# Attention with a paged cache: queries and own keys transposed in VectorE blocks and carried by the cached keys' copies, two pairs ahead, with the rope tables kept in DRAM

## The chip, the cores and the metric

The kernel runs on one core of a Trainium2 chip. The core's engines work side by side, each through its own list of instructions in order: TensorE (PE, with its weight loads shown as PEld), VectorE (DVE), ScalarE (ACT), GpSimd (POOL) and SyncE (SP), which here only issues DMA transfers. SBUF is the on-chip memory of 128 partitions, PSUM the memory that TensorE writes. The metric is the device time of one execution in microseconds.

## The reference, cut to what matters

A block on x of shape 8 x 128 x 512, all in float32. A first layer applies a weight matrix chosen for each batch row, then a causal attention with 32 heads of 16, and adds x. A second layer attends with 32 query heads and 8 key heads of 128 over 512 cached positions and the 128 own ones; then comes a feed-forward product with low-rank additions, and x is added again.

```python
q = _rmsnorm(q, q_norm_w)
k = _rmsnorm(k, k_norm_w)
q = _rope(q, pos)
k = _rope(k, pos)
kc = k_cache[block_table].reshape(bsz, L, HK, D)
vc = v_cache[block_table].reshape(bsz, L, HK, D)
k_all = jnp.concatenate([kc, k], axis=1)
v_all = jnp.concatenate([vc, v], axis=1)
scores = jnp.einsum('bqhd,bkhd->bhqk', q, k_all) * SCALE
scores = jnp.where(valid[:, None, None, :], scores, -1e+30)
probs = jax.nn.softmax(scores, axis=-1)
o = jnp.einsum('bhqk,bkhd->bqhd', probs, v_all)
```

The change touches the second attention: how rotated queries and own keys get their depth onto the partitions, as the score product needs it, and where the cosine and sine tables of `_rope` are kept.

## The kernel before, in words

**Stages.** Stage one (lines 276 to 801, up to about 220 us) computes the first layer, batch row by batch row, and prepares the second: rope tables (`angles`, `tables`), page indices, merged low-rank matrices (`merge_loads` and its followers). Stage two (from line 804) is the second attention with the feed-forward part.

**Units.** Stage two is cut into N = 64 units, one for each key head g and batch row b. Two units with neighbouring key heads and the same row are a pair: unit u = 2n + m is half m of pair n, and a gathered page of the cache holds both heads. Heads go in four groups of 16 units: units 0 to 15 have g = 0 or 1, and so on. A unit projects its queries (four heads, `q_matmul`) and own key and value (`kv_matmul`), computes scores against 512 cached and 128 own keys, softmax, values, and the output projection, which is added up over g in `y_acc`. Rows that have had their last head (g = 7, from unit 49 on) pass through `ffn_flip`, `ffn_lora` and `ffn`.

**The loop.** The order on every engine is the order of the code (`manual_schedule`); semaphores are derived from the tiles. Iteration u of the loop at line 1052 runs: `scores(u)`, with the query product of unit u + 1 between the four heads (`between`); `kv_matmul` and `kv_turn` of u + 1; `values(u - 1)`; `norms`, `queries` of u + 1; for odd u `turn_keys` of pair u // 2 + 2; the gathers on POOL; `out_proj(u - 1)`; `own_keys(u + 1)`; weight loads; the feed-forward part.

**Queries and own keys.** `q_turn` multiplies the projection in PSUM by the tables (three DVE operations), POOL adds the halves into `qa`, ACT squares for the norm; `kv_turn` does the same for the key, `ka`, and copies the value to `vo`. `norms` computes the reciprocal roots on POOL. `queries` transposes `qa` by four TensorE transposes against the identity and one ACT copy into `qT`; `own_keys` does one transpose and one copy into `kTo`. The score products of line 889 (cached keys) and 896 (own keys) take `qT` as stationary operand, loaded anew for each of the two passes of a float32 product.

**Cached keys.** `turn_keys(n)` has DVE transpose the gathered keys of pair n in blocks of 32 x 32 into `flk`, of which there is one buffer. `move_keys(n, a)` issues four transfers on SP that carry the blocks to their partitions in `kT2` (two buffers), in runs of 256 bytes. `pair_keys`, called after the third head of `scores`, issues eight of them in each unit, for the next pair. The first two pairs use TensorE instead (`keys`).

**Probabilities.** After the division DVE transposes each head's probabilities in blocks into `flips` (one buffer), and 16 transfers on SP carry them to `pT`, which `values` reads one iteration later.

**SP's queue.** In each iteration: eight kT moves, then 16 pT moves, then loads of weights or feed-forward rows if any are due. It is one queue in order; a transfer that waits holds the later ones.

**Buffers.** `tile_a` is a ring of 12 buffers of 2 KB a partition that serves stage one (gathered conditioning weights `cw`, the merge inputs `la`, `lb`, `las`, `lbs`, `gs`) and stage two (`sq`, `qa`, `qb`, `qT`, `oT` and others). A new tile waits until the oldest one's readers are done. The score and value products share two PSUM buffers (`p_sc`), so that the score product of a third head waits for the softmax pass (line 902) of the first.

## Time and profile before

| | |
|---|---|
| median of three runs | 1414.55 us (1414.14 to 1414.56) |
| profiled execution | 1423.96 us, span 1421.1 us |
| PE busy | 1391.5 us, 98% |
| DVE busy | 931.8 us, 66% |
| ACT busy | 655.9 us, 46% |
| POOL busy | 568.2 us, 40% |
| query transposes, L254 | 256, 38.5 us |
| own-key transposes, L271 | 64, 17.5 us |
| cached keys by DVE blocks, L840 | 120, 42.8 us |
| kT moves on SP, L853 | 480 of 32 KB |
| pT moves on SP, L936 | 1008 of 80 KB |

Busy time is the time in which an engine has an instruction running; instructions of TensorE overlap, so the distance between starts, not the duration, tells what one costs. A timeline line gives the start and length in microseconds, the engine, the line of the kernel, the operation, what it writes from what, its shapes and its count; in brackets stands the idle time before it and what ended it. A line of the windows view gives a stretch, its length, the busy time and count of PE, PEld, DVE, ACT and POOL, the granted TensorE clock (1.00 is full), the DMA share and GB/s.

### The profile page before, as it was taken

To read this page: it belongs to the slowest core of one execution; us is meant where nothing else is said; L and a number is where in the kernel's file an instruction comes from. 1 tells how busy PE (TensorE), PEld (TensorE's weight loads), DVE (VectorE), ACT (ScalarE), POOL (GpSimd) and SP (SyncE) were. 2 spreads that over 40 slices of the span, in tenths; PEclk is the share of its full clock that TensorE was granted. 3 is DMA by queue.
4 is the path that set the end of the run, shared out by engine and by line. 5 is a ranking of instruction groups with operands and counts; after the bars stand their busy time and mean duration, and the time that the engine had idled before them with its cause. 6 is when DMAs were issued, how large, how long until landed. Compare 5 with 4: busy or idle time off the path is not lost.

```text
span 1421.1 us, 20290 instructions
## 1 busy us (share of the span) xinstructions
PE 1391.5 (98%) x6244; PEld 898.5 (63%) x6244; DVE 931.8 (66%) x2266; ACT 655.9 (46%) x1520; POOL 568.2 (40%) x553
## 2 busy tenths in 40 slices
PE   6999989999999999999999999999999999999998
PEld 6877755566666666666666666666666665666555
DVE  5777846566666666666666666666666665666651
ACT  3555535444444444444444444444444444344431
POOL 5774342433333333333333333333333433343220
PEclk9999999999999999999999999999999999999999
DMA  6255013444444565444445654444456544444440
GB/s 198 75 164 183 31 37 104 129 117 118 119 115 119 161 193 151 119 119 119 119 119 159 196 148 119 118 119 119 121 160 192 152 117 136 131 111 112 115 111 30
DMA packets 156202, 180.26 MB, mean 127 GB/s; under 512 B 92416, under 2 KB 97792, under 8 KB 156096
## 3 DMA queue, kind: packets, MB, share of 16 engines
q1 hardware_dynamic: 140544, 134.39, 34.0%
q0 software_dynamic: 15552, 44.58, 10.8%
q8 instruction: 50, 0.82, 0.2%
q14 instruction: 56, 0.46, 0.1%
HBM read 75.83 MB, written 4.72 MB: 57 GB/s over the span
## 4 chain that ended last, share of the span: by engine, by line
PE 93%; DVE 2%; issue 2%; DMA 1%; ACT 1%; POOL 1%; SPq 1%; another core or an unknown queue 0%; DVEq 0%; POOLq 0%; ACTq 0%
PE op L963 19%; PE qp L177 15%; PE sc L889 15%; PE yp L982 15%; PE kvp L217 7%; PE sc L896 4%; PE fp L1044 2%; PE hp L514 2%; PE qTp L254 2%; PE pT1p L638 2%; PE qp L530 2%; PE att L673 2%; PE o L657 1%; PE sc L595 1%; PE kvp L545 1%
## 5 line engine op out<-in xcount | busy, mean ns | idle before, releaser
L902 DVE CUSTOM_DVE_ANT_0 pr<-sc,mask,nq 128x640 f32<-128x640 f32 x256 | 226.0, 884 | 144.2 <-PE sc L896 90.9
L912 ACT ACTIVATE pr<-pr,nm 128x640 f32<-128x640 f32 x256 | 211.8, 827 | 189.3 <-DVE nm L902 102.1
L889 PE MATMUL sc<-kT,qT 128*128 128x512 f32 x512 | 262.0, 593 | 0.0
L177 PE MATMUL qp<-wq,x1T 128*128 128x512 f32 x512 | 251.2, 593 | 0.0
L963 PE MATMUL op<-pT,vg 128*128 128x256 f32 x1024 | 242.0, 379 | 1.6 <-DMA pT<-fl 1.6
L203 POOL TENSOR_TENSOR qa<-qa,qb 128x512 f32<-128x512 f32 x64 | 81.8, 1278 | 375.2 <-DVE sums L879 375.2
L982 PE MATMUL yp<-wo,oT 128*128 128x512 f32 x504 | 229.2, 598 | 2.0 <-DVE oT L971 2.0
L963 PEld LDWEIGHTS op<-pT,vg 128*128 128x128 f32 x1024 | 193.9, 190 | 27.8 <-DVE sums L879 1.8
L880 ACT ACTIVATE pr<-pr,sums 128x640 f32<-128x640 f32 x256 | 208.4, 814 | 0.0
L883 DVE STREAM_TRANSPOSE fl<-pr 128x640 f32<-128x640 f32 x252 | 189.2, 808 | 0.0
L896 PEld LDWEIGHTS sc<-kTo,qT 128*128 128x128 f32 x512 | 96.4, 190 | 124.4 <-issue 119.2
L982 PEld LDWEIGHTS yp<-wo,oT 128*128 128x128 f32 x504 | 91.4, 191 | 95.1 <-issue 91.5
L160 POOL DMA_INDIRECT kg<-in_k_cache_dram,idx_kv x128 | 131.6, 1029 | 35.3 <-issue 34.8
L160 POOL DMA_INDIRECT vg<-in_v_cache_dram,idx_kv x128 | 128.6, 1005 | 37.8 <-issue 33.6
L889 PEld LDWEIGHTS sc<-kT,qT 128*128 128x128 f32 x512 | 87.7, 191 | 80.2 <-issue 77.8
L256 ACT COPY qT<-qTp 128x512 f32<-128x512 f32 x64 | 37.5, 586 | 205.3 <-PE qTp L254 204.7
L217 PEld LDWEIGHTS kvp<-wkv,x1T 128*128 128x128 f32 x512 | 97.3, 190 | 40.5 <-issue 30.1
L217 PE MATMUL kvp<-wkv,x1T 128*128 128x256 f32 x512 | 121.0, 379 | 0.0
L244 POOL TENSOR_TENSOR rs<-ss,minus_half 128x5 f32<-128x5 f32 x64 | 76.5, 1196 | 83.1 <-DVE ss L242 82.2
L177 PEld LDWEIGHTS qp<-wq,x1T 128*128 128x128 f32 x512 | 82.8, 191 | 31.5 <-issue 31.5
L896 PE MATMUL sc<-kTo,qT 128*128 128x128 f32 x512 | 99.2, 275 | 0.0
L273 ACT COPY kTo<-kTp 128x128 f32<-128x128 f32 x64 | 17.1, 267 | 166.4 <-issue 115.2
(155 smaller groups left out, 1701.1 us busy)
## 6 DMA issues: line engine op xcount, KB each, us to landing
pT<-fl SPq DMA_DIRECT2D x1008, 80.0 KB
kT<-flk SPq DMA_DIRECT2D x480, 32.0 KB
wq<-in_wq_dram SPq DMA_DIRECT2D x8, 1024.0 KB
wo<-in_wo_dram SPq DMA_DIRECT2D x8, 1024.0 KB
wkv<-in_wkv_dram SPq DMA_DIRECT2D x8, 512.0 KB
kg<-in_k_cache_dram,idx_kv POOLq DMA_INDIRECT x128
vg<-in_v_cache_dram,idx_kv POOLq DMA_INDIRECT x128
res<-x_kept SPq DMA_DIRECT2D x8, 256.0 KB
```

Source lines behind the costliest of these rows:

```text
L160: nc.gpsimd.indirect_dma_start(out=dst[:, c].rearrange("p n d -> p (n d)"), out_offset=None, in_=src, in_offset=bass.IndirectOffsetOnAxis( ...
L177: nc.tensor.matmul(s["qp"][:].rearrange("p h d -> p (h d)"), x1T[b][:, c, :], weights[g][0][:, c, :], start=(c == 0), stop=(c == KC - 1),)
L203: nc.gpsimd.tensor_tensor(qa[:], qa[:], qb[:], ALU.add)
L217: nc.tensor.matmul(s["kp"][:], x1T[b][:, c, :], weights[g][1][:, c, :], start=(c == 0), stop=(c == KC - 1))
L880: nc.scalar.activation(prs[r][:], prs[r][:], AF.Copy, scale=sums[:, r : r + 1])
L883: nc.vector.transpose(s["flips"][:, :, :, r, :].rearrange("p b c j -> p c b j"), prs[r][:])
L889: nc.tensor.matmul(sc[:, : NBLK * P].rearrange("p (k j) -> p k j", j=32), s["qT"][:, r, :], s["kT"], start=True, stop=True,)
L896: nc.tensor.matmul(sc[:, NBLK * P : NK], s["qT"][:, r, :], s["kTo"][:], start=True, stop=True)
L902: nc.vector.tensor_tensor_reduce(out=pr[:], in0=sc[:, :NK], in1=mask[:], scale=s["nq"][:, r : r + 1], scalar=3.0e38, op0=ALU.add, op1=ALU.min,
L912: nc.scalar.activation(pr[:], pr[:], AF.Exp, bias=nm[:, r : r + 1], scale=-1.0, accum_out=sums[:, r : r + 1],)
L963: nc.tensor.matmul(ops[h][:, : 2 * S], cached(u, "vg", c) if c < NBLK else s["vo"][:], s["pT"][:, :, c, 2 * h : 2 * h + 2, :].rearrange("p ...
L982: nc.tensor.matmul(yp[:], s["oT"][:, r, :], weights[g][2][:, r, :], start=(r == 0), stop=(r == REP - 1))
```

## The change

From pair 2 on (units 4 to 63) queries and own keys go the way of the cached keys. `flk` and `kT2` grow from 4 to 9 rows of blocks (`ROWS`): four for cached keys, four for the query heads, one for the own key. `turn_ahead(v)` adds two DVE block transposes that write unit v's queries, interleaved with those of its pair's other unit (a step of two elements), and its own key into `flk`. The eight transfers for a pair's half stay as many, each with 9 rows in place of 4. The score products read queries and own keys from `kT2`. TensorE transposes remain for units 1 to 3 (and unit 0 in stage one).

So that a pair is ready in time, projection runs four units ahead: iteration u projects u + 4; iteration 0 projects 1, 2 and 3, iteration 1 projects 4 and 5, and iterations 60 to 63 project nothing. Weights of queries and keys are loaded three iterations earlier.

The tables are no longer kept in SBUF: stage one builds them in `tab_all`, stores them to DRAM, and `load_tab` brings each pair's 256 KB back into one of two buffers. The `tile_a` ring shrinks to 9 buffers; `las`, `lbs` and `gs` get buffers of their own, and `vo`, `ka` and `nq` more buffers.

```diff
-        return both.tile(shape, F32, tag="a", name=name, bufs=12)
+        return both.tile(shape, F32, tag="a", name=name, bufs=9)
...
+    tab_kept = dram.tile([B, P, 4, D2], F32, tag="tab", name="tab_kept")
+    tabs = {}
...
+    def load_tab(n):
+        if n < N // 2:
+            tabs[n] = both.tile([P, 4, D2], F32, tag="tab", name=f"tab_{n}")
+            nc.sync.dma_start(out=tabs[n][:], in_=tab_kept[n % B])
...
-        flk = p2.tile([P, 4, NBLK, 2, 32], F32, tag="flk", name=f"flk_{n}", bufs=1)
+        flk = p2.tile([P, 4, ROWS, 64], F32, tag="flk", name=f"flk_{n}", bufs=1)
...
-        kT = p2.tile([P, NBLK, 4, 2, 32], F32, tag="kT2", name=f"kT2_{n}")
+        kT = p2.tile([P, ROWS, 4, 64], F32, tag="kT2", name=f"kT2_{n}")
...
+            s["kT"] = kT[:, :NBLK, :, own].rearrange("p c a i -> p (c a) i")
+            s["qT"] = [
+                kT[:, NBLK + r].rearrange("p a (i m) -> p (a i) m", m=2)[:, :, m] for r in range(REP)
+            ]
+            s["kTo"] = kT[:, NBLK + REP, :, own]
+
+    def turn_ahead(v):
+        flk, m = pairs[v // 2]["flk"], v % 2
+        nc.vector.transpose(
+            flk[:, :, NBLK : NBLK + REP, :].rearrange("p b r (i m) -> p r b i m", m=2)[:, :, :, :, m],
+            st[v]["qa"][:].rearrange("p r d -> p (r d)"),
+        )
+        nc.vector.transpose(
+            flk[:, :, NBLK + REP, 32 * m : 32 * m + 32], st[v]["ka"][:]
+        )
...
     def pair_keys(u):
         if u == 2:
-            turn_keys(u)
+            turn_keys(2)
+            turn_ahead(4)
         if 1 < u < N - 2:
+            if u % 2 == 0:
+                turn_ahead(u + 3)
             for a in range(u % 2 * 2, u % 2 * 2 + 2):
                 move_keys(u // 2 + 1, a)
...
+        ahead = {0: [1, 2, 3], 1: [4, 5]}.get(u, [u + 4] if u + 4 < N else [])
...
+        def project(v):
+            for c in range(KC):
+                q_matmul(v, c)
+            for part in q_turn(v):
+                part()
+            for c in range(KC):
+                kv_matmul(v, c)
+            kv_turn(v)
...
-            norms(u + 1)
-            queries(u + 1)
...
+            norms(ahead[0])
+        if u == 0:
+            queries(1)
+            keys(1)
+        if u == 1:
+            keys(2)
+            keys(3)
+        if u > 2 and u % 2 and u // 2 + 2 < N // 2:
+            turn_keys(u // 2 + 2)
+            turn_ahead(u + 3)
...
         if u == 0:
+            project(2)
             flip_last(x1_last)
...
-            own_keys(u + 1)
...
+            own_keys(1)
+            norms(2)
+            project(3)
+            queries(2)
+            own_keys(2)
+            norms(3)
+            load_tab(2)
+            load_tab(3)
             load_wo(1)
+        elif u == 1:
+            queries(3)
+            own_keys(3)
+            project(5)
+            norms(5)
+        if u % 2:
+            load_tab((u + 7) // 2)
```

## The prediction

> **What bounds the kernel now.** I read the page first, its busy times and the chain that ended last.
>
> ```profile
> span 1421.1 us, 20290 instructions
> ...
> PE 1391.5 (98%) x6244; PEld 898.5 (63%) x6244; DVE 931.8 (66%) x2266; ACT 655.9 (46%) x1520; POOL 568.2 (40%) x553
> ...
> PE 93%; DVE 2%; issue 2%; DMA 1%; ACT 1%; POOL 1%; SPq 1%; another core or an unknown queue 0%; DVEq 0%; POOLq 0%; ACTq 0%
> ```
>
> PE (TensorE) is the bound nearly everywhere: a microsecond taken from PE shortens the kernel, unless a wait takes its place. Next, the timeline of PE from the end of one unit of the second attention into the next.
>
> ```profile
> 719.46 0.60 PE L254 MATMUL qTp<-ident,qa 128*128 128x128 f32 x4
> 719.90 3.60 PE L982 MATMUL yp<-wo,oT 128*128 128x512 f32 x8
> 723.34 0.27 PE L271 MATMUL kTp<-ident,ka 128*128 128x128 f32 x1
> 723.45 1.02 PE L889 MATMUL sc<-kT,qT 128*128 128x512 f32 x2
> ...
> 726.47 1.02 PE L889 MATMUL sc<-kT,qT 128*128 128x512 f32 x2
> ```
>
> Starts follow each other without a gap. Four query transposes take 719.46 to 719.90, the own-key transpose 723.34 to 723.45. A unit repeats every 17.78 us (719.46, 737.25). Then the same stretch on DVE (VectorE).
>
> ```profile
> 722.01 1.42 DVE L840 STREAM_TRANSPOSE flk<-kg 128x256 f32<-128x256 f32 x4
> 723.54 0.69 DVE L989 TENSOR_TENSOR y<-yp,y 128x512 f32<-128x512 f32 x1
> 724.14 0.55 DVE L874 TENSOR_SCALAR mask<-place,lens_f 128x640 f32<-128x640 f32 x1
> 724.83 0.88 DVE L902 CUSTOM_DVE_ANT_0 pr<-sc,mask,nq 128x640 f32<-128x640 f32 x1
> 725.64 0.08 DVE L902 DVE_READ_ACCUMULATOR2_ANT nm<- 128x1 f32 x1
> ```
>
> After an odd unit DVE works without a pause from L840 to the first softmax pass (L902), which frees the scores' PSUM buffer at 725.72. The third score product needs that buffer and starts at 726.47: 0.75 us of slack, the tightest place of the loop. Last, three places where PE does stand still today: PE's timeline in unit 2 and in unit 63, with SP's timeline for the latter, and the granted clock by windows.
>
> ```profile
> 272.43 5.40 PE L982 MATMUL yp<-wo,oT 128*128 128x512 f32 x8 [2.00 <-DVE oT L971]
> ...
> 1386.44 1.97 PE L963 MATMUL op<-pT,vg 128*128 128x256 f32 x8 [1.57 <-DMA pT<-fl]
> ```
>
> ```profile
> 1374.22 10.25 SPq L936 DMA_DIRECT2D pT<-fl  x16
> ```
>
> ```profile
> 270.00:275.00 5.00, 3.00 (x9) 1.26 (x8) 3.21 (x11) 0.59 (x1) 2.33 (x3) 0.85 0.38 90
> 275.00:280.00 5.00, 5.00 (x15) 2.48 (x14) 1.99 (x4) 0.27 (x1) 3.23 (x4) 0.80 0.71 200
> ```
>
> Two things to keep: a 2.00 us stall was followed by a clock of 0.85 and 0.80, and the next output projection took 5.40 us in place of 3.60, so such a stall costs about 1.8 us again; and from SP's first pT issue to the value product are 12.2 us (1374.22 to 1386.44), sixteen issues of 0.63 us and the landing.
>
> **PE work removed.** L254 and L271 go for units 4 to 63 (1 to 3 keep them). 60 x (0.44 + 0.11) = 60 x 0.54 = 32.5 us, all on the path. ACT's two copies (0.59 + 0.27 us a unit) go too, off the path. Taken alone the unit becomes 17.24 us.
>
> **What replaces it on DVE.** Two block transposes a unit, 512 and 128 columns. Four L883 of 640 columns take 3.00 us, four L840 of 256 take 1.42; that gives a pitch of 0.73 and 0.34 us, 0.08 plus 1.02 ns a column, so 0.60 + 0.21 = 0.81 us. They write with a step of 8 bytes, for which there is no row; I bound them by 0.81 and twice that, and take 0.81, since no L840 or L883 row shows its many short runs costing extra. For odd units they run inside an even unit after the third softmax pass, in a 0.97 us idle stretch of DVE ahead of the fourth: hidden, and with that cover gone the fourth pass only moves into the 0.75 us that DVE idles before the next qp. For even units they stand right after L840, ahead of y, mask and the first softmax pass, in the stretch above. There PE comes 0.54 us earlier and DVE 0.81 us later: 0.75 - 0.54 - 0.81 = -0.60, with 0.06 us of hand-over a stall of 0.66 us. It needs L989 on DVE (for head group 0 ACT copies y, and there DVE idles a further 1.00 us, at 296.99) and no FFN behind the unit (its five products give PE 4.3 us, from 1316.73 to 1321.03). So units 17, 19 ... 49: 17 x 0.66 = 11.2 us lost; at twice the price 25 us.
>
> **Transfers and queues.** Each kT move grows from 128 to 288 packets of 256 bytes. The packet records put 128 in 0.31 us on 16 engines, so 288 in 0.70 us, against an issue pitch of 0.64 us; a unit's eight lag about 1 us at most. Engine time a unit: 1280 packets more at 17.5 ns over 16 engines, 1.4 us, in a stretch whose DMA share is 0.49. SP issues 16 x 0.633 + 8 x 0.64 us plus half a table load, 15.6 us of 17.24. The kT moves of an even unit now wait on SP for the odd unit's turn, about 1 us; behind them are that unit's pT moves, which have 2.5 us of SP idle before (715.5 to 718.0). Issue time does not follow packets: wq with 512 packets issues in 0.43 to 0.53 us, pT with 32 in 0.59. I take nothing; the other end is the third rival. The table load (256 KB for two units) is issued two units ahead and waits for nothing late. The weight loads move with their first use.
>
> [...]
>
> **Stationary queries with a step of 8 bytes.** Every load in the trace is contiguous (190 ns, a new one every 0.108 us behind 128-column passes). Ends: the same rate, 0; half rate, 0.108 us exposed at five loads a unit, 60 x 0.54 = +32 us. I take 0, as the moving kT, already cut in runs of 32, runs at the 593 ns of contiguous qp; that row has no step inside a run, so the other end stays a rival.
> [...]
>
> **The front.** Units 2, 3 and 5 are projected additionally in units 0 and 1: PE work that is only moved. In unit 1, norms(5) and the adds before it come on POOL behind rs(4) and eight gathers of 1.26 us. From the end of the value product: oT and rs(4) 1.9, gathers 10.1, qa, ka, rs 2.9, then nq, ka, mask and softmax on DVE 2.1, together 17.0 us until the buffer is free; PE needs it after key transposes 0.87, yp 3.44, queries 0.54, projection 5.16, two scores 2.15 and a qp pass 0.86: 13.0. So a stall of 4 us at unit 2, then about 1.4 at its yp because 2 x 0.81 us join L840 in the middle of the unit, and 2.2 of low clock; today 2.0 + 1.8 there and 1.3 in unit 0. Net +3, ends 0 and 6.
>
> **Stage one.** With 9 instead of 12 rotating buffers lb_1 to lb_3 wait on SP for the last conditioning (155.4 us, where las waits now), and w_eff and the gate rows queue behind them. DVE reads the gates at 161.6 and would wait some 2 to 3 us; PE has work queued. The 2 MB of tables leave at 92 us, in a slice where DMA is half busy. +2, ends 0 and 5.
>
> **The tail.** Units 60 to 63 project nothing, so PE's 5.16 us there no longer cover the pT moves. Without projection the probabilities are turned 10.45 us after a unit's first score (unit 63: 1379.67, divisions to 1388.4, then the last turns), plus 12.2: values may start 22.7 us after, and SP's kT moves make it 23.3 in unit 60. PE arrives in unit 61 after scores 4.6, values 4.3, yp 3.44, scores 4.6, yT 0.43: 17.4. Stall 5.9. Unit 62 has FFN work before it and waits for nothing; in unit 63 again 22.7 against 17.4, 5.3. Less today's 1.57: +9.6; DVE-bound scores +0.8; low clock after two stalls 2 x 1.8: +3.6. Together +14, ends 8 and 18.
>
> **Sum.** -32.5 + 11.2 + 3 + 2 + 14 = -2.3 us. In the profiled execution 1423.96 us (span 1421.1 and 2.9 around it) becomes 1421.7; that execution lies 9.4 over the median, so I apply the difference to the median: 1414.55 - 2.3, or **1412 us**.
>
> **Rivals.**
> 1. The stalls stay small (a softmax buffer freed in time, PE's stalls at front and tail half of mine, no low clock): 32.5 less about 10, 1392 us. For it: DVE is a third idle. Against: the odd boundary is DVE work end to end. 15%.
> 2. The stepped weight loads run at half rate: it decides once a load takes longer than the 0.108 us pass before it. 1412 + 32 = 1444 us, slower. 11%.
> 3. SP becomes the loop: kT issues at the pace of their packets or worse. It decides at 0.85 us an issue ((17.24 - 10.13 - 0.3) / 8); at 1.2 us a unit takes 20.0 and the kernel 1412 + 60 x 2.8 = 1580 us. Against: wq's issue time. 7%.
> 4. DVE writes with the step at half rate: 14 us more at the boundaries, 1426 us. PE's gain is then a DVE wait, and the change does not do what it says. 10%.
> Mine: 57%, 1412, its own range 1404 to 1420.
>
> **How the numbers follow.** Within 0.2% (2.8 us, about what a measurement of this kernel can tell) means 1411.7 to 1417.4. My case splits 26 / 15 / 16 into faster, same, slower; rival 1 adds 15 faster, rivals 2 and 3 18 slower, rival 4 nearly all slower: 0.41, 0.16, 0.43. The range leaves half of rival 1 below, rival 3 and part of 2 above: 1394 to 1446.
>
> **What would show it.** No L254 and L271 beyond units 1 to 3. Between an odd unit and the next, from unit 17, a gap of about 0.7 us before the third score, released by nm of L902; unit pairs of 35.1 us there and 34.5 in head group 0. PE waits on pT of 5 to 6 us in units 61 and 63, with low clock behind. Loads of the stepped queries at 190 ns. A kT issue of about 0.65 us. Wrong I would be if the loads lengthen, if SP shows no idle time, or if the boundary shows no gap.

## The result and the profile after

The changed kernel takes 1422.21 us (median of six runs, 1418.23 to 1424.01), the kernel before in the same comparison 1413.89 us (six runs, 1412.67 to 1414.56): a ratio of 1.0057, 95% interval 1.0043 to 1.0072, 8.3 us slower. Two repetitions on other chips gave 1.0081 (1.0065 to 1.0096) and 1.0054 (1.0038 to 1.0071). The time lies inside the predicted range (1394 to 1446), but the direction that the forecast leaned to, 2 us faster, is wrong.

The runs below fell on several chips, on which the kernel before took 1413.9 to 1422.6 us, so times are compared within one group of runs only, as ratios, and stretches of the loop by their length. A stretch is read from one profiled execution.

The page of the profile after, for the lines shown of before:

```profile
span 1418.9 us, 19695 instructions
...
PE 1370.0 (97%) x5944; PEld 873.0 (62%) x5944; DVE 977.5 (69%) x2386; ACT 598.2 (42%) x1400; POOL 557.9 (39%) x553
...
PE 65%; SPq 11%; DVE 10%; DMA 9%; issue 3%; POOL 1%; ACT 1%; DVEq 0%; POOLq 0%; ACTq 0%
```

300 matmuls are gone, and PE is busy 21.5 us less. But the chain that ended last, 93% PE before, is now 65% PE, and SP's queue (11%) and transfers (9%) have come in where they had 1% each. DVE rose from 2% to 10%. The rest of this section looks for the places.

**The boundary after an odd unit**, PE's timeline of the changed kernel, at the place that answers the one shown of before:

```profile
662.75 1.02 PE L935 MATMUL sc<-kT 128*128 128x512 f32 x2
663.61 0.39 PE L942 MATMUL sc<-kT 128*128 128x128 f32 x2
663.84 1.03 PE L935 MATMUL sc<-kT 128*128 128x512 f32 x2
...
664.93 1.02 PE L183 MATMUL qp<-wq,x1T 128*128 128x512 f32 x2
666.18 1.14 PE L935 MATMUL sc<-kT 128*128 128x512 f32 x2 [0.23 <-DVE nm L952]
```

and DVE's for the same stretch:

```profile
661.84 1.43 DVE L864 STREAM_TRANSPOSE flk<-kg 128x256 f32<-128x256 f32 x4
663.19 0.67 DVE L885 STREAM_TRANSPOSE flk<-qa 128x512 f32<-128x512 f32 x1
663.78 0.27 DVE L889 STREAM_TRANSPOSE flk<-ka 128x128 f32<-128x128 f32 x1
663.98 0.65 DVE L1039 TENSOR_TENSOR y<-yp,y 128x512 f32<-128x512 f32 x1
664.55 0.54 DVE L920 TENSOR_SCALAR mask<-place,lens_f 128x640 f32<-128x640 f32 x1
665.23 0.88 DVE L952 CUSTOM_DVE_ANT_0 pr<-sc,mask,nq 128x640 f32<-128x640 f32 x1
666.04 0.08 DVE L952 DVE_READ_ACCUMULATOR2_ANT nm<- 128x1 f32 x1
```

The two new transposes, L885 and L889, take 0.79 us from start to next start (663.19 to 663.98), the first softmax pass ends at 666.12, and the third score product starts at 666.18, released by it, 1.25 us after the product ahead of it where two passes back to back take 0.86 (662.75 to 663.61). These pairs repeat every 35.08 us (17.79 + 17.29); in head group 0 a pair takes 34.64 (17.35 + 17.29), against 35.72 before (17.93 + 17.79).

**The weight loads**, SP's timeline of the changed kernel. x8 is one unit's kT moves, x16 one unit's pT moves:

```profile
438.55 0.53 SPq L136 DMA_DIRECT2D wq<-in_wq_dram  x1
439.18 0.50 SPq L137 DMA_DIRECT2D wkv<-in_wkv_dram  x1
439.73 7.34 SPq L896 DMA_DIRECT2D kT<-flk  x8
447.18 10.30 SPq L986 DMA_DIRECT2D pT<-fl  x16
457.58 0.53 SPq L128 DMA_DIRECT2D tab<-tab_kept  x1
458.22 0.39 SPq L136 DMA_DIRECT2D wq<-in_wq_dram  x1
458.70 0.46 SPq L137 DMA_DIRECT2D wkv<-in_wkv_dram  x1
459.25 7.12 SPq L896 DMA_DIRECT2D kT<-flk  x8
466.48 10.60 SPq L986 DMA_DIRECT2D pT<-fl  x16
477.12 5.23 SPq L896 DMA_DIRECT2D kT<-flk  x8
```

SP goes from row to row without a gap from 438.55 to 482; what it waits lies inside the rows. Eight kT moves, 5.23 us at 477.12, take 7.34 and 7.12 us behind a weight load, and the unit from 447.18 to 466.48 costs SP 19.30 us, where PE's shortened unit is 17.3. PE's units there last 18.15 and 19.07 us. In this trace such long units stand in pairs at five of the six places where wq and wkv or wo of two heads are loaded (from 449, 539, 733, 1016 and 1105 us; none at the second loads of wo). There the loop of before has units of its ordinary length but for one, of 19.76 us, at the last loads of wo. What SP waited for in the loop (total us, times, longest):

```profile
SPq L986 <- DVE fl L929: 32.7, 37, 1.9
SPq L896 <- DVE flk L889: 16.3, 16, 2.4
...
SPq L896 <- DMA wkv<-in_wkv_dram: 6.3, 6, 1.6
SPq L896 <- DMA wo<-in_wo_dram: 5.9, 6, 2.3
```

In the traces of this kernel and of the one before, the kT move eight issues behind a load waits until the load has landed, though no data ties the two: here wkv, issued at 439.18, lands at 446.47, and the move eight issues behind it starts at 446.49, where SP was done with the one ahead at 445.64. All 18 kT moves that stand so behind a load in this trace start after its landing, 14 of them within 0.03 us. The wait is not new: before, all 18 start within 0.02 us of it. The same view of the kernel before:

```profile
SPq L936 <- DVE fl L883: 80.9, 39, 2.5
...
SPq L853 <- DMA wkv<-in_wkv_dram: 7.6, 6, 1.4
SPq L853 <- DMA wo<-in_wo_dram: 6.9, 6, 2.4
```

Before, SP waited 80.9 us for turned probabilities (`fl`): it had time left. After, it is 32.7 us, and 16.3 us go to a wait that did not exist, for `flk`, the turned queries and keys.

How PE comes to wait in the two units shown, 18.15 and 19.07 us long:

```profile
453.14 1.13 PE L935 MATMUL sc<-kT 128*128 128x512 f32 x2 [0.52 <-DVE nm L952]
478.80 1.96 PE L1013 MATMUL op<-pT,vg 128*128 128x256 f32 x8 [1.56 <-DMA pT<-fl]
```

The second is a value product whose pT moves are late. The first is a third score that waits for DVE, and DVE is late because `flk` has one buffer: the last kT move that reads it, issued at 446.49, lands at 448.93, and DVE's next transpose into it starts at 449.25, 0.80 us late. Over the whole run that line reads, after and, below, before:

```profile
L864 DVE STREAM_TRANSPOSE flk<-kg 128x256 f32<-128x256 f32 x120 | 42.8, 414 | 5.0 <-DMA pT<-fl 3.6
...
L840 DVE STREAM_TRANSPOSE flk<-kg 128x256 f32<-128x256 f32 x120 | 42.8, 413 | 2.0 <-DMA kT<-flk 0.4
```

(The line after names `pT`. In the stretch shown a pT move lands at 449.25, the very time at which DVE starts, and the last kT move out of `flk` at 448.93; the transpose shares no data with that pT move.) The kT moves are late because they land late behind a load: the fifth of the eight, issued at 442.54, lands at 448.22, after 5.7 us, where the median in the loop is 2.2.

**The front and the tail**, PE's timeline of the changed kernel:

```profile
277.04 2.08 PE L935 MATMUL sc<-kT,qT 128*128 128x512 f32 x2 [3.59 <-DVE nm L952]
290.11 3.67 PE L1032 MATMUL yp<-wo,oT 128*128 128x512 f32 x8 [0.54 <-DVE oT L1021]
...
1335.72 3.70 PE L1032 MATMUL yp<-wo,oT 128*128 128x512 f32 x8 [1.77 <-DVE oT L1021]
1347.33 2.67 PE L1013 MATMUL op<-pT,vg 128*128 128x256 f32 x8 [2.74 <-DMA pT<-fl]
...
1372.77 3.70 PE L1032 MATMUL yp<-wo,oT 128*128 128x512 f32 x8 [1.64 <-DVE oT L1021]
1384.29 1.97 PE L1013 MATMUL op<-pT,vg 128*128 128x256 f32 x8 [2.64 <-DMA pT<-fl]
```

with the granted clock (the number behind POOL's count) in two of these places:

```profile
275.00:280.00 5.00, 2.96 (x5) 1.60 (x6) 3.10 (x9) 2.45 (x5) 0.09 (x1) 0.67 0.00 0
...
1345.00:1350.00 5.00, 2.67 (x9) 2.26 (x10) 3.06 (x8) 3.45 (x7) 0.00 (x0) 0.84 0.59 117
```

To compare runs, the span is cut at the first score product of units 0, 4 and 60. "Front" contains three projections of 5.16 us that the change moved there from the tail (15.48 us).

| run | to unit 0 | front, 0 to 4 | loop, 4 to 60 | tail, 60 to end |
|---|---|---|---|---|
| before | 220.62 | 74.95 | 1025.46 | 100.06 |
| before, repeated (`b_again`) | 223.89 | 72.26 | 1027.01 | 100.06 |
| after | 218.15 | 92.73 | 1013.70 | 94.33 |
| after, repeated (`after_again`) | 224.61 | 93.72 | 1016.55 | 95.99 |
| after, repeated (`after_third`) | 225.50 | 94.19 | 1012.47 | 96.02 |

The loop lost 30.2 us of transposes (56 x 0.54) and got only 9 to 15 us shorter.

### The profile page after: what moved, and what is told of

Its sections match the earlier page's. It is cut to its first block, busy times and chain, and to the rows that moved or that the text cites. A ratio compares the mean times of both kernels' runs of the same rounds, so it can differ in the third digit from the quotient of the medians.

```text
span 1418.9 us, 19695 instructions
## 1 busy us (share of the span) xinstructions
PE 1370.0 (97%) x5944; PEld 873.0 (62%) x5944; DVE 977.5 (69%) x2386; ACT 598.2 (42%) x1400; POOL 557.9 (39%) x553
## 4 chain that ended last, share of the span: by engine, by line
PE 65%; SPq 11%; DVE 10%; DMA 9%; issue 3%; POOL 1%; ACT 1%; DVEq 0%; POOLq 0%; ACTq 0%
PE op L1013 13%; PE qp L183 11%; PE sc L935 10%; SPq L986 10%; PE yp L1032 8%; PE kvp L223 5%; DMA wkv<-in_wkv_dram 3%; PE sc L942 2%; DMA pT<-fl 2%; DVE fl L929 2%; DMA kT<-flk 2%; PE fp L1094 2%; PE hp L526 2%; PE pT1p L650 2%; PE qp L542 2%
## 5 line engine op out<-in xcount | busy, mean ns | idle before, releaser
L952 DVE CUSTOM_DVE_ANT_0 pr<-sc,mask,nq 128x640 f32<-128x640 f32 x256 | 223.4, 883 | 81.6 <-PE sc L942 71.2
L935 PE MATMUL sc<-kT 128*128 128x512 f32 x480 | 248.3, 599 | 8.8 <-DVE nm L952 7.5
L942 PEld LDWEIGHTS sc<-kT 128*128 128x128 f32 x480 | 94.2, 196 | 111.8 <-issue 111.8
L935 PEld LDWEIGHTS sc<-kT 128*128 128x128 f32 x480 | 87.3, 196 | 97.5 <-issue 61.4
L166 POOL DMA_INDIRECT kg<-in_k_cache_dram,idx_kv x128 | 123.9, 968 | 35.3 <-issue 34.6
L942 PE MATMUL sc<-kT 128*128 128x128 f32 x480 | 93.8, 277 | 0.0
L641 POOL TENSOR_TENSOR pr<-pr,sums 128x1024 f32<-128x1024 f32 x32 | 60.0, 1897 | 70.5 <-DVE sums L640 58.6
L630 ACT ACTIVATE pr<-sc,nm 128x128 f32<-128x128 f32 x256 | 67.7, 415 | 33.3 <-DVE nm L616 33.3
```

The costliest lines, as they stand in the source:

```text
L166: nc.gpsimd.indirect_dma_start(out=dst[:, c].rearrange("p n d -> p (n d)"), out_offset=None, in_=src, in_offset=bass.IndirectOffsetOnAxis( ...
L935: nc.tensor.matmul(sc[:, : NBLK * P].rearrange("p (k j) -> p k j", j=32), s["qT"][r], s["kT"], start=True, stop=True,)
L942: nc.tensor.matmul(sc[:, NBLK * P : NK].rearrange("p (a j) -> p a j", j=32), s["qT"][r], s["kTo"], start=True, stop=True,)
L952: nc.vector.tensor_tensor_reduce(out=pr[:], in0=sc[:, :NK], in1=mask[:], scale=s["nq"][:, r : r + 1], scalar=3.0e38, op0=ALU.add, op1=ALU.min,
```

## The experiments

Four questions, by size: the loads, the boundary, the removed work itself, and the two ends.

**Base.** The kernel before once more, and the changed kernel twice.

> The kernel before once more, to see what an ordinary execution of it looks like: its first profiled execution took 1423.96 us where its other runs took 1413 to 1414.6. Theory A (that profile held about 10 us of waits that ordinary executions don't have): this profile's span is 1410 to 1412 us, and against the first one the missing time shows in named places, unit 2 (2.0 us stall and 1.8 us of low clock) and stage one the first candidates. Theory B (the profiler itself adds the 10 us to this kernel): the span is again about 1421 us while the times are 1414 us.

Measured: 1421.77 us, ratio 0.9994 (0.9985 to 1.0004). The span is 1423.2 us where the other runs took 1420 to 1425, so neither theory holds here: on this chip every run is about as long as the first profiled one. The loop of before is the same in both traces but for units 49 and 50 (19.76 and 17.79 us, here 20.75 and 18.35). The front is not: the stall of 2.00 us and the slow output projection at 272.43, which the prediction showed as a standing cost, are absent here (a stall of 1.01 us, the projection at 3.70 us). They belonged to the profiled execution.

> The changed kernel unchanged, beside the kernel before on the same chip, as the base of this group. From the two traces the parts add up to -32.5 us (transposes), +8.5 (boundary), +10 (around the weight loads), +11.3 (tail), +2 to +5 (front), +3 (stage one): +2 to +5 us. The first comparison gave +8.3. If the parts are all of it, the difference here is +2 to +6 us; if a part is missing, it is +8 again.

Measured: 1432.74 against 1420.46 us, ratio 1.0081 (1.0065 to 1.0096): 11.5 us by the ratio. So the parts read from the first pair of traces were too small.

> The changed kernel unchanged, as the base beside the kernel before on this chip: +6 to +12 us, as in the two comparisons so far (ratios 1.0057 and 1.0081), with 8 to 13 us of excess around the weight loads in the loop from unit 4 to 60 (1011 to 1017 us).

Measured: 1429.38 against 1421.27 us, ratio 1.0054 (1.0038 to 1.0071), loop 1012.47 us.

**Do the weight loads cost 10 us, and how?** First the loads were taken away:

```diff
     def load_qkv(g):
+        if g > 1:
+            weights[g] = weights[g - 2][:2]
+            return
...
     def load_wo(g):
+        if g > 1:
+            weights[g].append(weights[g - 2][2])
+            return
```

> The changed kernel without the later loads of wq, wkv and wo: groups 2 to 7 use the weights of the group two before, so the output is not the reference's. Theories A and B: 10 us faster than the changed kernel, all pairs from unit 4 to 60 at 34.6 or 35.1 us. Theory C: no change, the long units stay. If A holds, the kernel with the loads on ACT's queue comes within 2 us of this one; if B, it does not.

Measured: 1419.68 us, ratio 0.9992 (0.9983 to 1.0001), 12.6 us less than the changed kernel in the same group (1.0081 less 0.9992, of 1420). The loop is 1003.64 us, and every pair from unit 4 to 50 has its length of 34.6 or 35.1 us but for one unit of 18.14. This loop is also, to 0.2 us, before's with two other steps applied: 1025.46 - 30.2 + 17 x 0.50 = 1003.8; that it fits so closely is in part luck, as before's loop holds 2.0 us at unit 49, and the changed kernel's units are 0.03 us longer than those of `no_turn` below (17.29 against 17.26). So the excess of the three runs of the changed kernel over it, 10.1, 12.9 and 8.8 us, is what the loads cost. Compared with `no_w` product by product, 5.4, 8.0 and 5.6 us of it stand ahead of value products (pT late) and 4.6, 4.9 and 3.1 us ahead of score products (in the main DVE late). Theory C falls.

The next two put the loads on another queue: `queue = nc.gpsimd if g > 1 else nc.sync` for the first, `nc.scalar` for the second, on wq, wkv and wo.

> The changed kernel with the later loads of wq, wkv and wo issued by POOL in place of SP. Theory A (at the weight loads SP's queue is what delays the pT moves: eight kT moves took 7.3 us there in place of 5.2): units around the loads go from 18.2 to 19.1 us back to 17.3 and 17.8, the time falls by about 8 us, ratio to the kernel before about 1.000. Theory B (the bytes of the weights delay the pT moves whoever issues them): no change, ratio 1.006.

Measured: 1463.43 us, ratio 1.0283 (1.0268 to 1.0298): units of up to 25.56 us where POOL issues a load. PE waits there for moves that SP issued:

```profile
457.60 3.75 PE L1015 MATMUL op<-pT,vg 128*128 128x256 f32 x8 [5.21 <-DMA kT<-flk]
```

POOL's two issues (0.84 and 0.83 us, from 446.24) are short. But the last two pT moves, which SP issued at 447.32 and 447.96, behind the loads, land at 455.14 and 457.04, after 7.8 and 9.1 us, where the median of pT moves in the trace of the changed kernel is 2.4. That fits theory B, by which the loads delay moves whoever issues them, and is far more than it forecast. How large that part is when SP itself issues the loads, ahead of its moves in one queue, this run does not tell.

> The changed kernel, but the later loads of wq, wkv and wo (groups 2 and up) are issued by ACT instead of SP. Theory A (these loads stand in SP's queue ahead of the kT and pT moves, which start late by their issue): units of 18.2 to 19.1 us beside the loads fall back to the 17.8 / 17.3 us of their neighbours, 8 to 10 us faster than the changed kernel. Theory B (their 1 to 2 MB occupy the DMA engines that the 256-byte packets of the kT moves need too, whoever issues them): the excess stays, within 2 us of the changed kernel. Theory C (the excess has nothing to do with the loads): the same as B, and no gain without the loads either.

Measured: 1491.24 us, ratio 1.0499 (1.0486 to 1.0513). What SP waited for in this kernel's loop:

```profile
SPq L988 <- DMA wo<-in_wo_dram: 40.3, 5, 9.1
...
SPq L988 <- DMA wq<-in_wq_dram: 21.5, 3, 8.8
SPq L898 <- DMA wq<-in_wq_dram: 17.3, 3, 6.0
```

SP's moves, which share no data with the weights, wait up to 9.1 us for loads that ACT issued; in the changed kernel, where SP issues the loads, its longest such wait was 2.3 us. So the wait that stood in SP's queue is still there, and longer; what lengthens it was not shown. Neither A nor B is tested by this run; it adds a cost of its own.

Then the loads stayed on SP, in pieces: two halves of wq and of wo and wkv by itself, one piece behind each group of four kT moves or behind eight pT moves.

```diff
                 move_keys(u // 2 + 1, a)
+                next_piece()
...
+            if a == 1:
+                next_piece()
```

> The changed kernel, but SP issues each later load of wq and wo in two halves and wkv by itself, one piece behind each group of four kT moves or behind eight pT moves, in place of 1.5 MB in one go ahead of the kT moves. Theory A (the kT moves wait behind a burst of 5 us of all DMA engines): long units shrink from 18.2 - 21 us to at most 0.5 us over their neighbours, 8 to 11 us faster than the changed kernel, so 0 to +3 us against before. Theory B (the same bytes cost the same wherever they stand, as the queue has no idle time): long units stay, +8 to +12 us against before.

Measured: 1427.83 us, ratio 1.0059 (1.0045 to 1.0073), loop 1011.79 us. `tail_split`, of the same group and with the loads as in the changed kernel, has a loop of 1011.40 us. The spreading brought nothing, as theory B expected. Theory A falls in the form in which I gave it.

A count fits that. Taken from the traces is the time from a unit's last pT issue on SP to the first value product that reads these probabilities; where PE waited for pT it had fallen to 2.3 to 2.7 us, which the landing then took (two numbers where even and odd units differ):

```
                     ordinary units      smallest, beside a load
before               5.4                 3.1
before, no turns     4.9                 2.2   (no_turn, below)
after, group 0       4.9 and 3.5 - 4.2   2.3, with PE waiting
after, later         5.4 and 3.7 - 4.9   2.5, with PE waiting
after, no loads      as after            3.0   (no_w)
```

Beside a load it is smaller by 2.3 us before and 2.7 in `no_turn`. On SP two loads cost about 3 us: 1.0 to 1.2 us of issue and about 2 us more for the eight kT moves behind them, half of which is the wait for the landing of wkv. Before, 5.4 us had room for that. The shorter unit alone takes 0.5 us, and in every second unit about 1 us more goes to the kT moves that wait for the turn (`flk`), ahead of the pT moves.

What of the change used the rest was asked by taking away the additional packets alone (`in_` and `out` of a move cut to the cached keys' rows, `:NBLK`), and the later table loads alone (`tabs[n] = tabs[3]` for n above 3).

> The changed kernel, but the kT moves carry only the cached keys (128 packets of 256 bytes, as before, in place of 288). The turned queries and own keys stay behind, and the scores read four rows of cached keys in their place with the same steps, so the output is not the reference's; turns on DVE, number of SP issues, tables and weight loads are those of the changed kernel. Theory P (the 160 additional packets a move hold the queue, so that behind a weight load the kT and pT moves land late): the excess around the weight loads (8 to 13 us) goes, the loop from unit 4 to 60 takes 1003 to 1005 us. Theory S (SP's issue time, with its waits for the landing of the weights, has too little slack in a unit of 17.3 us, whatever the packets): the excess stays, 1011 to 1017 us.

Measured: 1418.43 us, ratio 1.0023 (1.0010 to 1.0037), loop 1006.87 us: 3.2 us of excess instead of 8.8 to 12.9. At the first load a unit of 19.00 us stays.

> The changed kernel without the table loads behind the fourth: later pairs use the fourth pair's tables, so the output is not the reference's. SP has 0.26 us more a unit and the queue 1.0 us less of transfers every two units. Theory P: 1 to 2 us of the excess go, loop 1010 to 1014 us. Theory S: the slack grows from 1.7 to 1.9 us a unit, 2 to 4 us go, loop 1008 to 1013 us. If the table loads are the cause by themselves: 1003 to 1005 us.

Measured: 1420.88 us, ratio 1.0036 (1.0014 to 1.0058), loop 1007.13 us: 3.5 us of excess. The profiled execution took 1418.52 us, 2.4 less than the median, and by the ratio alone the gain is not clear of the changed kernel's 1.0054 and 1.0057.

In these traces each of the two takes away more than half, though neither is all of the cause. That fits a threshold: what one of them gives back keeps most units above the 2.3 to 2.7 us. It does not fit a theory in which the packets, or the tables, are the cost by themselves. How the excess divides between them, or between SP's issues, its waits and the bytes of the loads, can't be said from these runs.

The table loads alone, put into the kernel before (ring of buffers at 12, everything else as before):

```diff
-    ca = [one([P, B, D2], F32, f"ca_{n}") for n in range(2)]
-    sa = [one([P, B, D2], F32, f"sa_{n}") for n in range(2)]
+    tab_kept = dram.tile([B, P, 4, D2], F32, tag="tab", name="tab_kept")
...
+        if u % 2 == 0:
+            load_tab(u // 2 + 2)
```

> The kernel before with one part of the change: the rope tables kept in DRAM and loaded per pair by SP; the ring of buffers stays at 12, queries and keys are turned on PE as before. Theory A (the part costs only in stage one, by the order on SP's queue, and its loads hide later): +1 to +4 us, all of it before the first score of the second attention, units of 17.8 us as before. Rival (the 256 KB loads of SP disturb the loop by themselves): +5 us or more, with long units next to them.

Measured: 1424.34 us, ratio 1.0023 (1.0009 to 1.0037), +3.3 us. My theory A put all of it before the first score. Its loop, however, takes 1030.19 us, 3 to 5 us more than before's, with units of 18.74 and 23.54 us; the latter, which took 19.76 and 20.75 in the traces of before, begins beside SP issues of a table, wo and the feed-forward rows in one row (1103.03 to 1106.50). In this trace the tables cost something even with the long units, where SP has other loads to issue.

**The boundary.** The even unit's turn was moved to the next even unit, behind its second softmax pass:

```diff
+            if r == 1 and u % 2 == 0 and 2 < u < N - 2:
+                turn_ahead(u + 2)
...
-            turn_ahead(u + 3)
```

> The changed kernel with the even unit's block transposes taken from the end of the odd unit to the next unit, between its second and third softmax pass, where DVE idles 0.87 us. Theory A (after an odd unit DVE is the path, by 0.5 us, 17 times): pairs of units go from 35.08 to 34.6 us, the time falls by 8 us, ratio 1.000. Theory B (the 0.5 us come from PE's own operands, or DVE idle time at the new place isn't free): no change or a new stall in the middle of the unit, ratio 1.006 or more.

Measured: 1424.8 us, ratio 1.0012 (1.0001 to 1.0023). Pairs of 17.29 + 17.29 us from unit 19 on, away from the loads: the 0.50 us is gone, and the loop is 1003.80 us, 8.5 us over the ideal of 995.3 (1025.46 - 30.2); the long units beside loads hold about as much (19.28, 19.88 and 19.54 us the longest). The profiled execution, at 1419.12 us, was faster than the median. This is the best version that computes everything, and no faster than the kernel before.

**Is the removed work really on the path?** The kernel before, with the transposes left out and nothing in their place:

```diff
     def queries(u):
         s = st[u]
+        if u > 3:
+            s["qT"] = s["qa"]
+            return
...
     def own_keys(u):
         s = st[u]
+        if u > 3:
+            s["kTo"] = s["ka"]
+            return
```

> The kernel before, with the query and own-key transposes and ACT's copies of them left out for units 4 to 63 and nothing in their place: the scores read queries and keys as they lie, not turned, so the output is not the reference's. Theory A (PE is the bound and each transpose is on its path): 60 x 0.54 = 32.5 us faster than before, units of 17.25 us. Rival (other waits take the freed time even without any replacement: pT moves or the softmax buffer): clearly less, 10 to 25 us, with PE waits in the loop.

Measured: 1393.12 us, ratio 0.9807 (0.9795 to 0.9820), 27.4 us faster than before. Units of 17.26 us as expected, among them those beside the loads of wq and wkv. The 5 us that miss to 32.5 are lost from 1052 to 1109 us (units of 17.97, 19.03 and 19.44 us, loop 998.38 instead of 995.3) and in the tail, which did not get shorter (100.65). Before itself loses 2.0 and 3.0 us at unit 49, there in a wait for `qa`. In `no_turn` PE waits there for moves, 1.61 us for kT and 1.27 for pT: a shorter unit runs into SP's queue in one place even without any replacement.

**The tail.** Two attempts by the order of work and by ACT's queue, and one with POOL's. The first put the feed-forward part of iterations 61 and 63 ahead of the value products (`early = u in (N - 3, N - 1)`):

> The changed kernel with the feed-forward products of iterations 61 and 63 ahead of the value products in place of behind the output projection; the same work. Theory A (in the tail PE waits for the pT moves, 2.7 and 2.6 us, because units 60 to 63 project nothing): the two waits are filled, and with them the low clock after the first, 5 to 7 us less, ratio 1.001. Theory B (the tail is bound by the chain of moves itself, whatever PE does meanwhile): no change, ratio 1.006.

Measured: 1436.44 us, ratio 1.0102 (1.0087 to 1.0117), tail 98.59 us. The pT waits are gone, and in their place PE waits 7.8 us in two pieces (3.92 and 3.91) for ACT's copy of `yT`. The second changed one line, `queue = nc.scalar if u >= N - 4 and k % 2 else nc.sync`, for the pT moves:

> The changed kernel, with half of the pT moves of the last four units issued by ACT. Theory A (in the tail the pace of SP's issues sets the value product): sixteen issues shrink to eight, the two pT waits of 2.7 us go and the low clock behind them, 6 to 9 us faster than the changed kernel. Rival (the turns on DVE or the landing set it): 0 to 3 us faster. A wait of one queue for the other's landings may appear.

Measured: 1429.92 us, ratio 1.0066 (1.0054 to 1.0078), tail 98.03 us, none of the gain. One pT wait of 4.95 us instead of two of 2.7, a new one of 2.70 us for ACT, and SP waits 10.3 us in two pieces for pT landings, as the expectation's last sentence feared.

Three repairs together (pieces, this split, the moved turn):

> Three repairs together on the changed kernel: weights in pieces, half of the last pT moves on ACT's queue, and the even unit's turn moved behind the second softmax pass of the next even unit. If the three losses are separate: 9 + 7 + 8 = 24 us faster than the changed kernel, 12 to 16 us faster than before. If they hide each other: less than 18 us faster than the changed kernel.

Measured: 1423.53 us, ratio 1.0022 (1.0013 to 1.0031). Of three losses only the boundary was mended; the pieces and the split each failed, as above.

The last run left the weights alone, moved the turn, issued the later tables on ACT and gave POOL a quarter of the last pT moves (`queue = nc.gpsimd if u >= N - 4 and k == 3 else nc.sync`):

> Three repairs on the changed kernel, none of which leaves work out: the even unit's turn behind the second softmax pass of the next even unit, the table loads issued by ACT instead of SP, and a quarter of the pT moves of the last units issued by POOL. If the losses are what the earlier runs showed: boundary 8 us, 3 to 5 us of the excess around the weight loads, 2 to 5 us in the tail, 13 to 18 us faster than the changed kernel and 2 to 8 us faster than the kernel before. Rival: a queue that waits for the other's landings (as with the weights on ACT's queue) gives it back, and it is no better than the repair of the boundary alone (+1 to +2 us against before).

Measured: 1439.68 us, ratio 1.0138 (1.0121 to 1.0155). The tail is 89.91 us, 6.1 us shorter than in `after_third` but 3.1 shorter than in `both_even` (93.04), which has the same pT waits of 2.74 and 2.64 us and no low clock behind them. The two value products now wait 0.75 us each: the pace of SP's issues was the cause of most of those waits. The loop is 1023.26 us, 11 us longer although the boundary was mended, for this reason (SP's waits in this kernel):

```profile
SPq L991 <- DMA tab<-tab_kept: 41.5, 19, 4.2
```

pT moves on SP wait for tables that ACT issued, 41.5 us in all, though no data ties the two. The rival of the expectation holds.

**Fewer and larger packets, with the result kept.** The moved tile was laid out anew: queries, keys and own keys interleaved with a step of 18 elements over the tokens, so that a kT move is 32 runs of 2304 bytes.

```diff
-        kT = p2.tile([P, ROWS, 4, 64], F32, tag="kT2", name=f"kT2_{n}")
+        kT = p2.tile([P, 4, 32, 2 * ROWS], F32, tag="kT2", name=f"kT2_{n}")
...
+            flat = kT[:].rearrange("p a i x -> p (a i) x")
+            s["qT"] = [flat[:, :, 2 * r + m] for r in range(REP)]
```

> The changed kernel with another layout of the moved tile: keys, queries and own keys interleaved with a step of 18 elements (72 bytes) over the tokens, so that each kT move is 32 packets of 2304 bytes in place of 288 of 256; the output is the reference's, SP issues as many moves, PE reads keys and stationary queries with a step of 72 bytes. Theory P: the excess goes, loop 1003 to 1005 us, 9 to 13 us faster than the changed kernel. Theory S: the loop stays at 1011 to 1017 us. If PE pays for the 72-byte step (moving or stationary), all units lengthen equally, by 0.5 us or more.

Measured: 1710.21 us, ratio 1.2081 (1.2056 to 1.2106). The units are 22.53 us, and 22.60 and 27.80 where others had 17.35 and 22.55. The two score lines of this kernel, the new layout and, below, the first four units with contiguous operands (minimum, median and maximum ns):

```profile
L935 PEld LDWEIGHTS sc<-kT x480: 301/304/310, 313.2 to 1670.7; 128*128 128x128 f32 x160
L935 PE MATMUL sc<-kT x480: 1117/1141/1141, 313.6 to 1671.6; 128*128 128x512 f32 x160
...
L935 PEld LDWEIGHTS sc<-kT,qT x32: 186/190/337, 220.3 to 301.4; 128*128 128x128 f32 x32
L935 PE MATMUL sc<-kT,qT x32: 592/592/1061, 220.3 to 301.8; 128*128 128x512 f32 x32
```

PE pays for the step of 72 bytes with almost twice the time of a pass, 1141 ns against 592. With units that long SP has time to spare, so the run says nothing on the loads.

> The interleaved layout of the run before, and the even unit's turn moved behind the second softmax pass of the next even unit. If packets (P) and the boundary are both gone: loop 995 to 997 us, 17 to 21 us faster than the changed kernel, 5 to 12 us faster than the kernel before. Under S: 8 us faster than the changed kernel, no better than the kernel before.

Measured: 1709.59 us, ratio 1.2072 (1.2049 to 1.2095): the same, for the same reason.

## Why the prediction was wrong

Step by step, in the order of its sum; the measured sizes come from the table of stretches, with 0.54 us for each unit whose transposes left the stretch (one in the front, three in the tail) and the three moved projections taken out, and from the runs named.

| step | predicted | measured |
|---|---|---|
| PE transposes removed | -32.5 | 0.54 a unit, as predicted; alone -27.4 (`no_turn`) |
| DVE at the boundary | +11.2 | +8.5 (17 x 0.50) |
| transfers and queues | 0 | +8.8 to +12.9 |
| stepped stationary loads | 0 | 0 |
| front | +3 | +2.8 in the first pair, +5.5 to +7.0 against before's other run |
| stage one | +2 | -2.5 in the first pair, +2.1 to +4.7 within a later group |
| tail | +14 | +11.4 to +13.0 |

**The failing step is "Transfers and queues", where "I take nothing".** Everything that makes the loss was on the table there: 15.6 of 17.24 us of SP's time in a unit, the kT moves of even units that wait for the turn, and a sentence on the loads that looked only at their place ("The weight loads move with their first use"). What the step left out is that a unit with a load isn't the average unit. It costs SP 19.3 us, about 1.0 us for two more issues and about 2 us more for the kT moves behind them, half of it in waits for a load's landing. These waits stood in the trace of before (7.6 and 6.9 us in SP's waits), and I left them out of the sum. It also left out that the kT moves behind a load land late, and that `flk`, with one buffer, hands this on to DVE and by the third score to PE, at a place where the boundary had used up the 0.75 us of slack. Taking the loads away returns 12.6 us by the medians, which is more than the whole loss. Rival 3, SP becomes the loop, named the right queue with the wrong mechanism, place and price: it isn't the issue time of a kT move (0.65 us, as predicted, far from the 0.85 at which it decides), it is the units beside loads.

**The boundary** was right: the gap stands where it was said, from unit 17, released by L952 (L902 before), and group 0 has none. It cost 0.50 instead of 0.66 us a pair. Pairs of 35.1 and 34.6 us were forecast at 35.1 and 34.5. The repair in `both_even` removes it. Rival 4 (the step makes DVE's writes slow) is out: L885 takes 0.68 us, forecast 0.60 in pitch and measured 0.59 (663.19 to 663.78).

**The stepped stationary loads** cost next to nothing: 196 ns against 190, and the passes behind each other as before; the whole unit is 0.03 us longer than in `no_turn`, whose loads are contiguous. Rival 2 is out. The step of 8 bytes is free to within this; with one of 72 (`kt_uniform`) a load takes 304 ns, and a pass 1141 instead of 592. No run has a step between the two.

**The busy shares** (PE 98%, DVE 66%) spoke for moving the transposes. PE did win its 0.54 us a unit and DVE did hold the two transposes nearly hidden. But shares of two engines left out the third party, the queue that carries what DVE turns: after a TensorE transpose one copy by ACT puts the result where it's needed, while the blocks that DVE turns are moved to their partitions by SP's queue (480 kT moves). By the medians (1413.89 against 1422.21 us) the transposes were better left on TensorE in this kernel.

**The tail** came out as predicted, 14 against 11.4 to 13.0, with half the mechanism. The pT waits in units 61 and 63 are 2.74 and 2.64 us, not 5 to 6; 1.77 and 1.64 us are waits of the output projection on DVE's copy `oT` in units 60 and 62, which were not forecast. A low clock followed one of the pT stalls in the first trace (0.84), both in `after_third` (value products of 3.39 and 2.81 us instead of 1.97) and none in `both_even`, so this term varies by execution. `best3` shows that most of the pT part goes when SP has a quarter less to issue.

**The front** was mis-sized by what it was compared with. The 2.00 us stall and the slow projection that I subtracted as today's cost are not in the second trace of before (1.01 and 3.70 us): a feature of one execution. The third score's wait of 3.59 us was forecast at 4.

**Stage one** stays somewhat open. Within a group, kernels with stage one as it was reach unit 0 at 223.89 (`b_again`) and 220.24 us (`no_turn`), those with the changed one at 226.0 to 228.1 and at 224.2 to 225.0. In the first pair it was the other way round, 218.15 after against 220.62 before. `tab_only`, with the 2 MB store of the tables and the ring of twelve, gets there at 221.54, where the changed kernel's versions of its group take 224.4 to 224.7: so there about 3 us go to the rest of the change in stage one, the ring of nine buffers with it, and not to the store.

The sum with the measured sizes, middle values taken (stage one from the later groups): -32.5 + 8.5 + 10.6 + 6.2 + 3.5 + 12.5 = +8.8 us, against +8.3, +11.5 and +7.7 us measured. That it comes so close is in part luck, as the terms are from several executions that differ by more. And `no_turn`, which brings only 27.4 alone, shows that they are not fully separate; part of the 10.6 would be lost to the shorter unit in any case.

A second reason for caution was in my own working: the profiled execution of before lay 9.4 us over its median, and I assumed that this excess was spread where it does not matter. 2.7 us of it were in the front (74.95 against 72.26), inside a term of the sum. Where the rest was stays open; on the chip of `b_again` all runs of before took about that long (median 1422.61 us).

## What to carry to other kernels

When a unit of a loop gets shorter, count every queue's time in the fullest unit, the one with the weight loads, not in the average one, and read the queue's own waits in the profile before: the 14 us that SP waited for loads to land were free only because each unit had 2.5 us to spare. An engine's idle share says that there is room for work; whether the data it produces has a way to its reader is a separate budget. And to put loads on a second queue is no cure by itself: look whether the first queue's moves then wait for their landing (up to 9.1 us in `w_act`), and whether the moves land late beside the load (after 7.8 and 9.1 us in `w_pool`).

## What the hardware showed that was not expected

- Moves on SP waited for the landing of loads that ACT issued, up to 9.1 us for 1 MB (`w_act`) and 4.2 us for 256 KB (`best3`), although no data ties them. The loop became 63 us longer than the changed kernel's in the one case (1079.55 against 1016.55) and 11 in the other. Half of the pT moves of four units on ACT's queue did the same on a smaller scale (10.3 us in the tail).
- Moves behind or beside a load landed late: kT moves on SP after 2.2 us (median), but after up to 8.5 us in the changed kernel with its loads and 3.9 without them (`no_w`); behind loads issued by POOL two pT moves took 7.8 and 9.1 us (`w_pool`).
- A float32 operand of TensorE with a step of 8 bytes was nearly free as stationary one (196 against 190 ns); with 72 bytes (`kt_uniform`) a stationary load took 304 ns and a moving pass of 512 columns 1141 instead of 592. DVE's block transpose of 512 columns took 0.68 us with writes 8 bytes apart and 1.12 us with 72.
- 256-byte runs between partitions cost little each: a move with 288 of them had an issue pitch of 0.65 us against 0.64 for 128 and landed after 2.2 us against 1.9 (medians). Behind loads the longest landing was 8.5 us with 288 and 7.5 with 128 (`no_move`), and without them the excess beside the loads fell by more than half.
